# Linear attention with a gate, LoRA experts and Strassen products in one program: when masks, weights, decays and gates are loaded or computed, the order of the inner products, and which rows of out_w are loaded ahead

## The chip, the cores and the metric

The kernel runs on one core of one Trainium2 chip. The metric is the time of one execution on the device, in microseconds (us), lower is better. Times are medians of several runs; next to them stands one execution that the hardware profiler recorded, with a span and a time of its own. All data is float32.

## The reference, cut to what matters

x is 2 x 512 tokens of 512 features. After a layer norm, two branches are computed and added to x: a linear attention with decay (32 heads of 128, gated), and a dense layer with 8 LoRA experts of rank 16, of which the router takes 2 for each token. Cut down:

```python
qkv = silu(xn @ qkv_w.T)                       # 1024 tokens x 12288: q, k, v of 32 heads
def step(kv, blk):                             # over blocks of 32 tokens
    scores = einsum('bhnd,bhmd->bhnm', cq, ck) * diag_decay
    intra = einsum('bhnm,bhmd->bhnd', scores, cv)
    inter = einsum('bhnd,bhde->bhne', cq * q_decay, kv)
    kv_next = kv * block_decay + einsum('bhnd,bhne->bhde', ck * k_decay, cv)
    return kv_next, intra + inter
xf = attn * rsqrt(mean(attn * attn) + EPS)     # over all 4096 features of a token
gate = sigmoid(xn @ gate_w.T)                  # 1024 x 4096
attention = gate * (norm_w * xf) @ out_w.T     # 1024 x 4096 times 4096 x 512
out = x + attention + base(xn) + experts(xn)
```

Nearly all the arithmetic lies in five products: q, k, v and gate (each 1024 x 512 times 512 x 4096), and the last one with out_w (1024 x 4096 times 4096 x 512).

## The kernel before, in words

**Two-level fast products.** The four projections are computed by a scheme of seven products in place of eight, on two levels. The output features are cut into 16 sets n: eight for v and gate in turn (n < 8, kind 0 and 1) and eight for q and k (kind 2; one set holds four heads). A set has seven outer rounds q (1 to 7), each a combination of a set's weight blocks with a combination of xn; a round has seven inner products i (1 to 7), each four 128x256 matmuls on TensorE (`inner_product`, L292, matmuls L300 and L303). That makes 112 rounds.

- The *weights*: `load_block` (L132) loads a block of 512 KB as two DMAs of 256 KB, into a ring of five buffers `raw`. `encode` (L151) is a generator on POOL: the outer combinations L156 (128x1024) into `s`, and four inner ones (L175 to L181) into `e`. It runs two rounds ahead of its products, one step per slot.
- The *evictions*: `after(r, i)` (L336) combines a product's result out of PSUM. Products 1 and 2 accumulate into one bank `pa`, 5 and 3 into `pc`, 6 into `pb`, 7 and 4 into `pd`. After product 1, ACT copies `pa` to `pb` (L375) before product 2 adds to `pa` and product 6 to `pb`; after product 6, ACT copies `pb` to `pd` (L386) before 7 and 4 add to `pd`. Other results are added to partial sums of earlier rounds in `outer_sums`, on DVE: `put` (L354), `taken` (L369), and the one after product 7 that makes `w2` (L395). In round q = 7 the `w2` is then added twice by `put`, into the partial sum u3 and into the finished quarter (1, 1).
- A finished quarter goes through `result` (L322): Silu (L328) or Tanh (L326) on ACT. v and gate are then written to DRAM (`v_kept`, `gate_kept`). q and k stay in `qk`, a ring of five buffers; when both halves of a head and batch are there, `complete` (L474) makes an *item* of it, 64 in all.

**Attention.** `attend` (L482) is a generator for one item. Its first four steps are DMAs and one DVE operation: load the head's decays as `mask` (L488, L489: two tiles of 64 KB each, ring of four), transpose k in 32x32 blocks on DVE (L494), write them to DRAM as `k_kept` (L497), load them back as `kt` (L502, four DMAs) and load v (L504). `complete` puts these steps 1, 2, 3 and 6 slots after the item is done (L479). Then come four stages:

- A: four score matmuls (L509, bank `sc`), times the mask on DVE (`scores`, L511), the decayed q on POOL (`qd`, L514), the load of the gate (L517);
- B: the decayed k on ACT (`kd`, L521), scaled by a column of the mask;
- C: three matmuls kd by v (L527, bank `sc`), their running sums on DVE (`state`, L529 and L531);
- D: seven matmuls into bank `at` (`pa`, L537 and L539); ACT squares them into `sq` (L545), POOL adds that to `ssq` (L546), DVE multiplies with the gate (`gT`, L548). Two slots later gT is written to DRAM as `g_kept` (L550).

`stages` (L556) interleaves the items: A of item i is followed by B and C of item i - 1 and D of item i - 2, where A and B share one step of the order, and C and D have one each.

**The order.** The main loop (L667 to L721) writes the order by hand. Slot k belongs to round r0 = k // 7 and place m = k % 7; `SLOTS` (L664) names for each place how many rounds back and which inner product. A slot first issues the weight loads (at m = 0 of a set's rounds q = 5, 7 and 3 the next set's blocks are loaded, two or four DMAs in one go), then the steps that are `later`, then the inner product with its evictions, then one step of `encode`, and last a stage of attention whenever a credit that grows by 24/49 a slot has reached 1. From the first q/k round on ((VG, 1), about 406 us into the span) up to the end of the early output products (L752) this written order is each engine's order (`manual_schedule`); before and after it, a scheduler orders the instructions. Each engine works its own queue in order. All DMAs go out from SP's queue in that order too, so a DMA that waits holds the DMAs behind it.

**Output projection.** It uses seven products on one level, over 16 pairs of heads p, for two halves f of the tokens. Per pair: out_w is loaded (512 KB, L586) and scaled by norm_w on ACT (L593), the attention result is loaded (`gated`, L598), and four sums each are formed of both (`gsum` on DVE, L609; `wsum` on POOL, L610); each product is two matmuls of 128x256 (L627). Four pairs (`EARLY`) begin while attention still ends: `ENDS` (L635) has their loads by slots, L736 to L746 runs the last stages of attention with pair 3's out_w scaled at the second (`left == 1`), and the sums of pairs 1 to 3. After the written order ends, the buffers of attention are given up and a pool `gated_pool` opens, into which pairs 4 and on are loaded (L764 to L766), then the products 2, 3 and 4 of pairs 0 to 3 run. x_back (2 MB, x plus the expert branch) is loaded into a pool that opens where the buffers of the projections were (L775 to L778), at pair 8 of the first half (L816), for the last additions (L787).

Of the kernel before, what the change touches and what calls it, by code (L numbers as in the profile page):

```python
# [60 lines left out]
def attn_moe_kernel(ctx: ExitStack, tc: tile.TileContext, x, qk_w, v_w, gate_w, out_w, norm_w,  # L61
# [70 lines left out]
    def load_block(n, fo, ko):  # L132


        t = blocks[n, fo, ko] = aw.tile([P, 2, 2, 256], F32, tag="raw", name="raw", bufs=5)
        ks = slice(2 * ko, 2 * ko + 2)
        for i in range(2):
            if kind(n) == 0:
                nc.sync.dma_start(t[:, i], v_w[n - n % 2 + i][:, ks, fo * 256 : (fo + 1) * 256])
            elif kind(n) == 1:  # L140
                h = 4 * (n - n % 2) + 4 * i + 2 * fo
                nc.sync.dma_start(t[:, i], gate_w[h : h + 2, :, ks, :].rearrange("f p k d -> p f (k d)"))
            else:
                nc.sync.dma_start(t[:, :, i, :],
                                  qk_w[4 * (n - VG) + 2 * fo + i][:, :, ks, :].rearrange("p u k d -> p u (k d)"))

# [51 lines left out]
    with tc.tile_pool(name="setup", bufs=1, side="right") as sp:  # L198
# [9 lines left out]
        load_block(0, 0, 0)  # L208
        nc.sync.dma_start(wbase, base_w)
        for fo, ko in ((1, 0), (1, 1), (0, 1)):  # L210
            load_block(0, fo, ko)
        load_block(1, 0, 0)
# [97 lines left out]
    qk = {}  # L310

    def place(n, fo, to, ij):

        fi, ti = divmod(ij, 2)
        if kind(n) < 2:
            return ring("v")
        item = 4 * (n - VG) + 2 * fo + fi, to
        if item not in qk:
            qk[item] = ring("qk", [P, 2, S])
        return qk[item][:, :, ti * HB : (ti + 1) * HB]  # L320
# [15 lines left out]
    def after(r, i):  # L336
# [5 lines left out]
        def put(ij, v, more):  # L342

            for (_, to), t in zip(adds, more):
                new = isinstance(to, str)
                o = outer_sums[n, to][ij] if new else place(n, *to, ij)

                def halves(t):
                    return t.rearrange("p (u y) -> p u y", u=2) if len(o.shape) == 3 else t

                if t is None:
                    nc.scalar.copy(o, v)
                else:
                    nc.vector.tensor_tensor(o, halves(v), halves(t), ALU.add)  # L354
                if not new:
                    result(n, *to, ij, o)
# [27 lines left out]
        elif i == 6:  # L384
            st["pd"] = seeded[1 + r % 2]
            nc.scalar.copy(st["pd"], st["pb"])  # L386
            st["w"] = taken("w", st["pb"], 1)
        elif i == 3:
            put(1, st["pc"], st["w"])
        elif i == 7:  # L390
            if len(adds) == 1:
                put(3, st["pd"], st["y"])
            else:
                c = temp("w2")
                nc.vector.tensor_tensor(c, st["pd"], st["y"], ALU.add)  # L395
                put(3, c, addends(3))
        elif i == 4:
            put(2, st["pd"], addends(2))
# [83 lines left out]
    def attend(head, b):  # L482
# [3 lines left out]
        mask = work.tile([P, 2, P], F32, tag="mask", name="mask", bufs=4)  # L486

        nc.sync.dma_start(mask[:, 0, :], decay[head][:, :P])  # L488
        nc.sync.dma_start(mask[:, 1, :], decay[head][P - 1, P : 2 * P].partition_broadcast(P))  # L489
# [13 lines left out]
        v = ring("v")  # L503
        nc.sync.dma_start(v, v_kept[s_][:, u, f, b, :])  # L504
# [30 lines left out]
        for j in range(TB):  # L535
            o = pa[:, j * P : (j + 1) * P]
            mm(o, v[:, j * P : (j + 1) * P], sc[:, j, :], True, j == 0)  # L537
            if j:
                mm(o, state[:, j - 1, :], qd[:, j - 1, :], False, True)  # L539
        if b not in seen:  # L540
# [6 lines left out]
        gT = ring("gT")  # L547
        nc.vector.scalar_tensor_tensor(gT, gate, 1.0, pa, ALU.add, ALU.mult)  # L548
# [7 lines left out]
    def stages():  # L556


        for i in range(ITEMS + 2):
            if i < ITEMS:  # L560
                while i not in ready or ready[i] > now[0]:
                    yield None
                next(running[i])
            if 1 <= i <= ITEMS:
                next(running[i - 1])
            if i < ITEMS:
                yield True
            if 1 <= i <= ITEMS:
                next(running[i - 1])
                yield True  # L570
            if i >= 2:
                next(running[i - 2])
# [91 lines left out]
    SLOTS = ((0, 1), (0, 5), (0, 2), (1, 7), (0, 6), (0, 3), (1, 4))  # L664
    credit = 0.0
    in_order = ctx.enter_context(ExitStack())
    for k in range(7 * len(rounds) + 7):  # L667
        now[0] = k
        r0, m = divmod(k, 7)
        if m == 0:  # L670
# [12 lines left out]
            if r0 < len(rounds):  # L683
# [13 lines left out]
                if n + 1 < NSET:  # L697
                    for fo, ko in {5: ((0, 0),), 7: ((1, 0), (1, 1)), 3: ((0, 1),)}.get(q, ()):
                        if (n + 1, fo, ko) not in blocks:
                            load_block(n + 1, fo, ko)  # L700
# [3 lines left out]
        if r0 == len(rounds) and SLOTS[m][0] == 0:  # L704
            if m == 0:
                sums[0].update({1: bank("fr"), 6: bank("fr"), 5: seeded[0], 7: seeded[1]})
            early_product()
        back, i = SLOTS[m]
# [9 lines left out]
        if items:  # L718
            credit = min(credit + 24 / 49, 1.5)
            if credit >= 1 and next(stage):  # L720
                credit -= 1  # L721
# [14 lines left out]
    for left, _ in enumerate(stage):  # L736
# [3 lines left out]
        if left == 1:  # L740
            scale_out_w(3)
        for _ in range(2 if left == 0 else 1):
# [21 lines left out]
    load_gated(0, EARLY)  # L764
    for p in range(EARLY, EARLY + 2):
        next_out_w(p, gated_pool)  # L766
# [8 lines left out]
    last_products.close()  # L775
    projections.close()
    late = right("late")
    x_back = late.tile([P, NT, HID], F32, tag="x_back", name="x_back")  # L778
# [30 lines left out]
    for i, (f, p) in enumerate(todo):  # L809
        if i + 1 < len(todo):  # L810
# [5 lines left out]
        if (f, p) == (0, NP // 2):  # L816
            nc.sync.dma_start(x_back, x_kept)
# [71 lines left out]
```

## Time and profile before

| what | value |
|---|---|
| runs | 1183.01, 1188.82 and 1192.49 us; median 1188.82 us |
| profiled execution | 1193.15 us, span 1191.4 us |
| mean granted clock of TensorE | 0.995 |
| ACT: Silu of q and k, L328 | 128 times, 630 ns each |
| ACT: copy `pa` to `pb`, L375 | 112 times, 575 ns each |
| ACT: copy `pb` to `pd`, L386 | 112 times, 575 ns each |
| DVE: gT, L548 | 64 times, 684 ns each |
| DVE: `w`, L369 | 110 times, 688 ns each |
| POOL: ssq, L546 | 62 times, 1272 ns each |
| POOL: qd, L514 | 64 times, 1017 ns each |
| POOL: outer combinations, L156 | 32 times, 2366 ns each |
| POOL: idle before qd, ended by the mask's DMA | 45.4 us in all |
| DVE: idle before gT, ended by ACT's square | 81.6 us in all |
| DMA: moved by all queues | 197.15 MB, mean 165 GB/s |
| DMA: weights of q and k, 64 issues of 256 KB | 4.9 us median from issue to landing |

The durations are means of one instruction in the profiled execution. "Idle before" is time in which the engine stood, put down to what ended the wait; it costs time only where TensorE then has to wait too. Queue time of an engine or of its instruction sequencer is written with a q or the ending ld: SPq is the queue from which DMAs are issued, PEld is the loading of matmul weights, which runs beside the matmuls. `ps_fr`, `ps_sc`, `ps_at` and `sd` are PSUM banks: two, two, one and three of them.

### The profile page before, as it was taken

To read this page: it belongs to the slowest core of one execution; us is meant where nothing else is said; L and a number is where in the kernel's file an instruction comes from. 1 tells how busy PE (TensorE), PEld (TensorE's weight loads), DVE (VectorE), ACT (ScalarE), POOL (GpSimd) and SP (SyncE) were. 2 spreads that over 40 slices of the span, in tenths; PEclk is the share of its full clock that TensorE was granted. 3 is DMA by queue.
4 is the path that set the end of the run, shared out by engine and by line. 5 is a ranking of instruction groups with operands and counts; after the bars stand their busy time and mean duration, and the time that the engine had idled before them with its cause. 6 is when DMAs were issued, how large, how long until landed. Compare 5 with 4: busy or idle time off the path is not lost.

```text
span 1191.4 us, 18113 instructions
## 1 busy us (share of the span) xinstructions
PE 1144.7 (96%) x6024; PEld 994.0 (83%) x6024; DVE 759.9 (64%) x1350; ACT 435.1 (37%) x772; POOL 737.7 (62%) x798
## 2 busy tenths in 40 slices
PE   6999999999999999999999998999989989899998
PEld 5578888888888878989989897988979878788887
DVE  7477766666675666667767766676666753636333
ACT  3244444434534434344343433434333431330000
POOL 5266977757767656657576765757766544655452
PEclk9999999999999999999999999999999999999999
DMA  7335465344444345555656656565566672864221
GB/s 242 114 107 183 153 212 194 127 157 161 142 140 151 124 145 172 167 177 173 193 178 188 180 156 207 158 194 164 168 199 168 214 226 91 328 212 125 89 89 53
DMA packets 188717, 197.15 MB, mean 165 GB/s; under 512 B 50128, under 2 KB 159696, under 8 KB 188368
## 3 DMA queue, kind: packets, MB, share of 16 engines
q1 hardware_dynamic: 188624, 195.98, 52.5%
q8 instruction: 49, 0.80, 0.3%
q14 instruction: 44, 0.36, 0.1%
HBM read 126.16 MB, written 69.76 MB: 164 GB/s over the span
## 4 chain that ended last, share of the span: by engine, by line
PE 67%; DVE 8%; DMA 6%; issue 3%; ACT 3%; SPq 2%; POOL 2%; DVEq 0%; ACTq 0%; POOLq 0%
PE ps_fr L303 14%; PE sd L303 13%; PE sd L627 5%; PE ps_at L89 5%; PE ps_sc L89 5%; PE sd L300 5%; PE ps_fr L627 4%; PE ps_sc L627 4%; PE ps_sc L303 4%; PE ps_fr L300 3%; DMA mask<-in_decay 3%; PE ps_sc L300 3%; DVE qk L354 2%; DVE sum L354 2%; PE ps_at L627 1%
## 5 line engine op out<-in xcount | busy, mean ns | idle before, releaser
L328 ACT ACTIVATE qk<-qk 128x512 f32<-128x512 f32 x128 | 80.6, 630 | 252.6 <-DVE qk L354 252.5
L303 PE MATMUL sd<-xt,e 128*128 128x256 f32 x672 | 166.8, 381 | 0.0
L546 POOL TENSOR_TENSOR ssq<-ssq,sq 128x512 f32<-128x512 f32 x62 | 78.9, 1272 | 126.4 <-ACT sq L545 116.9
L303 PEld LDWEIGHTS sd<-xt,e 128*128 128x128 f32 x672 | 125.1, 192 | 15.0
L369 DVE TENSOR_TENSOR w<-sd,sum 128x512 f32<-128x512 f32 x110 | 74.4, 688 | 72.0 <-ACT sd L386 71.0
L548 DVE SCALAR_TENSOR_TENSOR gT<-gate,ps_at 128x512 f32<-128x512 f32 x64 | 43.8, 684 | 89.4 <-ACT sq L545 81.6
L514 POOL TENSOR_TENSOR qd<-qk,mask 128x384 f32<-128x384 f32 x64 | 65.1, 1017 | 47.8 <-DMA mask<-in_decay 45.4
L610 POOL TENSOR_TENSOR wsum<-wo 128x256 f32<-128x256 f32 x56 | 46.2, 841 | 74.6 <-PE sd L627 34.6
L175 POOL TENSOR_TENSOR e<-s 128x256 f32<-128x256 f32 x64 | 46.8, 730 | 70.4 <-PE sd L303 49.9
L89 PE MATMUL ps_at<-scores,v 128*128 128x128 f32 x512 | 89.2, 277 | 0.0
L375 ACT COPY sd<-ps_fr 128x512 f32<-128x512 f32 x112 | 64.4, 575 | 48.2 <-PE ps_fr L300 23.4
L609 DVE TENSOR_TENSOR gsum<-gated 128x256 f32<-128x256 f32 x56 | 26.9, 521 | 85.0 <-PE ps_sc L627 71.1
L89 PEld LDWEIGHTS ps_at<-scores,v 128*128 128x128 f32 x512 | 78.2, 193 | 3.4
L156 POOL TENSOR_TENSOR s<-raw 128x1024 f32<-128x1024 f32 x32 | 75.7, 2366 | 2.7 <-DMA raw<-in_v_w 2.7
L303 PE MATMUL ps_fr<-xsum,s 128*128 128x256 f32 x288 | 75.4, 385 | 1.0 <-ACT sd L375 0.9
L89 PE MATMUL ps_at<-qd,state 128*128 128x128 f32 x384 | 74.6, 276 | 0.0
L386 ACT COPY sd<-sd 128x512 f32<-128x512 f32 x112 | 64.4, 575 | 23.0 <-PE sd L303 17.2
L175 POOL TENSOR_TENSOR e<-raw 128x256 f32<-128x256 f32 x48 | 35.6, 741 | 59.5 <-PE sd L303 32.6
L89 PEld LDWEIGHTS ps_sc<-qk 128*128 128x128 f32 x512 | 67.8, 193 | 3.4
L89 PE MATMUL ps_sc<-qk 128*128 128x128 f32 x512 | 68.0, 276 | 0.0
L303 PE MATMUL ps_fr<-xt,e 128*128 128x256 f32 x224 | 58.2, 382 | 9.8 <-DVE qk L354 9.8
L326 ACT ACTIVATE v<-v 128x512 f32<-128x512 f32 x64 | 40.4, 631 | 73.7 <-DVE v L354 69.1
(299 smaller groups left out, 2888.3 us busy)
## 6 DMA issues: line engine op xcount, KB each, us to landing
v_kept<-v SPq DMA_DIRECT2D x64, 256.0 KB, 2.5
gate_kept<-v SPq DMA_DIRECT2D x64, 256.0 KB, 2.5
raw<-in_qk_w SPq DMA_DIRECT2D x64, 256.0 KB, 4.9
v<-v_kept SPq DMA_DIRECT2D x64, 256.0 KB, 2.9
gate<-gate_kept SPq DMA_DIRECT2D x64, 256.0 KB, 3.9
g_kept<-gT SPq DMA_DIRECT2D x64, 256.0 KB, 3.5
gated<-g_kept SPq DMA_DIRECT2D x28, 512.0 KB, 3.7
k_kept<-squares SPq DMA_DIRECT2D x64, 192.0 KB, 4.1
```

What stands on the lines that cost most here:

```text
L89: nc.tensor.matmul(o, lhsT, rhs, start=start, stop=stop)
L156: nc.gpsimd.tensor_tensor(t, a, b, op)
L175: nc.gpsimd.tensor_tensor(e[:, 0], a21, a22, ALU.add)
L300: nc.tensor.matmul(o.rearrange("p (g j d) -> p j g d", g=2, j=2)[:, u], x_[:, u * P : (u + 1) * P], a, start=first and u == 0, stop=True, ...
L303: nc.tensor.matmul(o[:, u * HB : (u + 1) * HB], a[:, u], x_, start=first and u == 0, stop=True, skip_group_check=True)
L328: nc.scalar.activation(v, v, AF.Silu)
L369: nc.vector.tensor_tensor(o, v, t, ALU.add)
L375: nc.scalar.copy(st["pb"], st["pa"])
L386: nc.scalar.copy(st["pd"], st["pb"])
L514: nc.gpsimd.tensor_tensor(qd, q[:, P:].rearrange("p (j n) -> p j n", j=TB - 1), mask[:, 1, :].unsqueeze(1).to_broadcast([P, TB - 1, P]), A ...
L546: nc.gpsimd.tensor_tensor(ssq[b], ssq[b], sq, ALU.add)
L627: nc.tensor.matmul(sums[n][:, i * HO : (i + 1) * HO], l[:, i * P : (i + 1) * P], r, start=p == 0 and i == 0, stop=p == NP - 1, skip_group_ ...
```

## The change

It has eight parts. In the diff, the first `yield` stands in the loop over a block's two DMAs.

1. *Weights by halves.* `load_block` becomes a generator that yields after each DMA of 256 KB; the main loop takes one at each even place m, in place of up to four at m = 0.
2. *Masks.* An item's mask is loaded in `place`, when its first result gets its buffer, and no longer by `attend`'s first step after both results are there.
3. *v.* v is loaded in `attend`'s first step, where the mask was, and no longer after kt.
4. *SLOTS.* Product 7 of the round before moves one place ahead of product 2: 1, 5, 7, 2, 6, 3, 4 in place of 1, 5, 2, 7, 6, 3, 4.
5. *Decays ahead of products.* A slot that will run stage B (kd on ACT) issues it ahead of its inner product and evictions; A, C and D stay behind them. In `stages`, B is now taken on the first `next`, the rest on the second, told apart by `yield False`.
6. *Gates ahead of squares.* In stage D, gT on DVE is issued before ACT's square. Both read the bank `at`.
7. *One addition on POOL.* In round q = 7, the addition of `w2` to u3 runs on POOL; both of its inputs are in SBUF. It runs 16 times.
8. *Six pairs preloaded.* In the last stages, pair 3's out_w is scaled at `left == 5` in place of `left == 1`; there out_w of pairs 4 and 5 is loaded, into a pool that exists already, and pair 4's `gated` into a `raw` buffer. The pools of the projections are closed at pair 6 in place of ahead of the loop, and x_back is loaded there in place of at pair 8; its memory is then that of buffers which pair 4's products and sums still use.

```diff
 def load_block(n, fo, ko):
...
+            yield
+    def load_blocks(n, *of):
+        for fo, ko in of:
+            if (n, fo, ko) not in blocks:
+                yield from load_block(n, fo, ko)
...
+    def load_mask(head):
+        mask = work.tile([P, 2, P], F32, tag="mask", name="mask", bufs=4)
+        nc.sync.dma_start(mask[:, 0, :], decay[head][:, :P])
+        nc.sync.dma_start(mask[:, 1, :], decay[head][P - 1, P : 2 * P].partition_broadcast(P))
+        return mask
...
         if item not in qk:
             qk[item] = ring("qk", [P, 2, S])
+            masks[item] = load_mask(item[0])
...
-        def put(ij, v, more):
+        def put(ij, v, more, in_sbuf=False):
...
-                    nc.vector.tensor_tensor(o, halves(v), halves(t), ALU.add)
+                    engine = nc.gpsimd if new and in_sbuf else nc.vector
+                    engine.tensor_tensor(o, halves(v), halves(t), ALU.add)
...
-                put(3, c, addends(3))
+                put(3, c, addends(3), in_sbuf=True)
...
-        mask = work.tile([P, 2, P], F32, tag="mask", name="mask", bufs=4)
-        nc.sync.dma_start(mask[:, 0, :], decay[head][:, :P])
-        nc.sync.dma_start(mask[:, 1, :], decay[head][P - 1, P : 2 * P].partition_broadcast(P))
+        mask = masks.pop((head, b))
+        v = ring("v")
+        nc.sync.dma_start(v, v_kept[s_][:, u, f, b, :])
         yield
...
-        v = ring("v")
-        nc.sync.dma_start(v, v_kept[s_][:, u, f, b, :])
...
+        gT = ring("gT")
+        nc.vector.scalar_tensor_tensor(gT, gate, 1.0, pa, ALU.add, ALU.mult)
         if b not in seen:
...
-        gT = ring("gT")
-        nc.vector.scalar_tensor_tensor(gT, gate, 1.0, pa, ALU.add, ALU.mult)
...
         for i in range(ITEMS + 2):
             if i < ITEMS:
                 while i not in ready or ready[i] > now[0]:
                     yield None
-                next(running[i])
             if 1 <= i <= ITEMS:
                 next(running[i - 1])
             if i < ITEMS:
+                yield False
+                next(running[i])
                 yield True
             if 1 <= i <= ITEMS:
+                yield False
                 next(running[i - 1])
                 yield True
             if i >= 2:
+                yield False
                 next(running[i - 2])
...
-    SLOTS = ((0, 1), (0, 5), (0, 2), (1, 7), (0, 6), (0, 3), (1, 4))
+    SLOTS = ((0, 1), (0, 5), (1, 7), (0, 2), (0, 6), (0, 3), (1, 4))
...
-                if n + 1 < NSET:
-                    for fo, ko in {5: ((0, 0),), 7: ((1, 0), (1, 1)), 3: ((0, 1),)}.get(q, ()):
-                        if (n + 1, fo, ko) not in blocks:
-                            load_block(n + 1, fo, ko)
+                weights = load_blocks(n + 1, *{5: ((0, 0),), 7: ((1, 0), (1, 1)), 3: ((0, 1),)}.get(q, ())
+                                      if n + 1 < NSET else ())
+        if m % 2 == 0:
+            next(weights, None)
...
+        begun = None
+        if items:
+            credit = min(credit + 24 / 49, 1.5)
+            if credit >= 1:
+                begun = next(stage)
         back, i = SLOTS[m]
...
-        if items:
-            credit = min(credit + 24 / 49, 1.5)
-            if credit >= 1 and next(stage):
-                credit -= 1
+        if begun is False:
+            next(stage)
+            credit -= 1
...
-    for left, _ in enumerate(stage):
+    for left, _ in enumerate(begun for begun in stage if begun):
...
-        if left == 1:
+        if left == 5:
             scale_out_w(3)
+            for p in (4, 5):
+                load_out_w(p, early_pool.tile([P, 2, HID], F32, tag=f"wo{p}", name="wo"))
+            load_gated(0, 4, end_buffer("raw", [2, B, HT]))
...
-    load_gated(0, EARLY)
-    for p in range(EARLY, EARLY + 2):
-        next_out_w(p, gated_pool)
+    for p in (4, 5):
+        scale_out_w(p)
...
-    last_products.close()
-    projections.close()
-    late = right("late")
-    x_back = late.tile([P, NT, HID], F32, tag="x_back", name="x_back")
...
     for i, (f, p) in enumerate(todo):
+        if (f, p) == (0, 6):
+            last_products.close()
+            projections.close()
+            late = right("late")
+            x_back = late.tile([P, NT, HID], F32, tag="x_back", name="x_back")
+            nc.sync.dma_start(x_back, x_kept)
...
-        if (f, p) == (0, NP // 2):
-            nc.sync.dma_start(x_back, x_kept)
```

More of the change, by code (lines that the diff above doesn't have):

```diff
@@ L207, in attn_moe_kernel @@
                 nc.sync.dma_start(wra, router_a_w)
-        load_block(0, 0, 0)
+        for _ in load_block(0, 0, 0):
+            pass
         nc.sync.dma_start(wbase, base_w)
-        for fo, ko in ((1, 0), (1, 1), (0, 1)):
-            load_block(0, fo, ko)
-        load_block(1, 0, 0)
+        for _ in load_blocks(0, (1, 0), (1, 1), (0, 1)):
+            pass
+        for _ in load_block(1, 0, 0):
+            pass
         nc.sync.dma_start(nw, norm_w)
@@ L309, in attn_moe_kernel @@
              2: [("x1", (0, 0))], 3: [("u4", (0, 1))], 4: [("u3", (1, 0))]}
-    qk = {}
+    qk, masks = {}, {}
+    def load_mask(head):
[3 more added lines that the diff above has]
+        return mask
     def place(n, fo, to, ij):
```

## The prediction

> **What bounds the kernel now.** First the page, part 1: TensorE is the full engine, the others have room.
>
> ```profile
> PE 1144.7 (96%) x6024; PEld 994.0 (83%) x6024; DVE 759.9 (64%) x1350; ACT 435.1 (37%) x772; POOL 737.7 (62%) x798
> ```
>
> Busy time hides short stalls, so I read matmul starts in the timeline. Back to back, a 128x256 matmul starts 0.216 us after the last (a product has four: 0.86 us), a 128x128 one 0.112, a 128x512 one 0.429, a 128x136 one 0.116. At that pace 4032, 1832 (with the 16 of one column), 80 and 64 of them need 1119.6 us. Added up over the trace, start to start, 56.9 us go beyond that pace: 3.1 before 56 us (setup), 9.2 up to 406 us (v and gate sets), 31.7 up to 960 us (q/k sets with attention), 12.8 up to 1020 us (passage to the output projection), none afterwards. No edit can win more than this. By what ended them: ACT's copy L375 21.4 (8.1 in the v/gate part, 13.1 in the q/k part, 0.2 in setup), DVE's additions L354 11.8, ACT's kd L521 5.2, POOL's wsum 3.3, the scaled out_w (L593) 3.3, other DVE work 2.3, a v load 0.8, no semaphore 8.8 (part of it half clock). The waits of TensorE name the same ones (total, times, longest):
>
> ```profile
> PE ps_fr L303 <- ACT sd L375: 9.9, 12, 2.0
> PE ps_fr L303 <- DVE qk L354: 9.8, 6, 3.3
> PE ps_fr L627 <- ACT wo L593: 3.0, 1, 3.0
> PE ps_sc L89 <- ACT kd L521: 2.5, 2, 2.1
> ```
>
> Why is DVE late? The chain of waits at 503 to 515 us (start, length, what):
>
> ```profile
> 503.24 0.55 SPq L144
> 503.78 0.04 issue
> 503.83 0.61 SPq L144
> ...
> 505.79 7.15 DMA mask<-in_decay
> ...
> 513.03 0.06 DVE scores L511
> 513.10 0.55 issue
> 513.64 0.68 DVE sum L354
> 514.32 0.61 DVE qk L354
> 514.93 0.14 issue
> 515.07 2.60 PE ps_fr L303 x8
> ```
>
> Four weight loads of 256 KB go out in one burst, the mask queues behind them and lands 7.15 us after issue, L511 holds DVE, DVE's additions come late, and TensorE waits for their bank. The timeline of the passage shows the other kind:
>
> ```profile
> 977.79 1.33 ACT L593 ACTIVATE e<-e,nw 128x512 f32<-128x512 f32 x2 [6.13 <-DMA e<-in_out_w]
> 980.15 0.74 PEld L89 LDWEIGHTS ps_sc<-v,kd 128*128 128x128 f32 x6 [2.46 <-ACT kd L521]
> ```
>
> ACT stands 6.13 us before the scaling of pair 3's out_w, and square and kd behind it in its queue hold TensorE.
>
> **The change part by part.** The sum starts from the profiled execution: 1193.15 us (span 1191.4 and 1.75 around it), 4.3 above the median of the runs shown, 1188.82.
>
> *Product 7 moved (SLOTS).* Product 2 accumulates into the bank that L375 copies (575 ns); between products 1 and 2 lay product 5 alone, 0.86 us; now 7 too, 1.73 us. Cutting each stall by 0.86 leaves 2.8 of the 21.4. I take 17 off, 1.6 less than that, for the ACT delay below; bounds 0 (the copy is late anyhow) and 21.4. Product 2's result, its DVE addition (0.69) and Silu (0.63) come a slot later; its bank is wanted again three products (2.6 us) on: nothing. POOL waits for product 7 before it refills an operand buffer (L175 <- L303 and L300, 117 us in all); that ends a slot sooner, off the path: nothing.
>
> *Masks.* Same 128 DMAs of 64 KB, issued with the first result instead of a slot after the second: 3 slots earlier for one head of a pair, 5 for the other. A slot of the q/k part is 554 us / 392 = 1.41 us, so 4.2 and 7.1 us earlier, against longest waits of 6.2 (POOL) and 4.0 (DVE). The four buffers are held longer: the load now comes at least 6 slots (8.5 us) behind the kd of the item four back, for the last two items 1 and 0, where SP, and the k_kept, kt and weight loads behind it, may stand up to 1.4 us. Of the 10.7 us that DVE's additions cost in the q/k part I take 9.5; bounds 0 and 10.7.
>
> *Weights by halves.* The four 256 KB issues (2.5 us of SP at once) go to slots 0, 2, 4, 6: this helps the masks. The last half leaves 8.5 us later; its first use is 8 slots (11 us) after that, its landing 4.9. Only set 1 of the first two uses it in the next round; POOL stood idle 3.5 and 4.0 us there. Nothing; bounds 0 and 4.9.
>
> *v loads* move on SP from behind kt to before k_kept; their buffer was freed at least 7 slots before. The one stall on v goes: 0.8; bounds 0.8 gained and, by one 0.43 us issue ahead of 64 kt groups if all show, 28 lost. I take the gain: kt waits for k_kept's landing anyway (177 us of SP).
>
> *kd ahead of the product's evictions.* In the q/k part kd costs TensorE 2.9; I take 2.4. From kt's landing to kd's start the trace has 1.0 us at the lowest quartile and 2.3 in the middle; moved up by one or two evictions of 0.6, some 16 of 64 kd would hold ACT up to 1.0 us, with the L375 and L386 copies behind, which now have 1.73 us. Bounds 2.9 gained, 16 lost.
>
> *Gate ahead of square.* Both read one PSUM bank and the program orders them. DVE no longer waits for ACT (81.6 us, 51 times); ACT waits for DVE. By the trace the square starts 0.1 us (median) after the last matmul of its bank; then it needs DVE's 0.69 first: 0.7 later, 1.2 with the 0.47 that DVE is busy on average. Behind it on ACT stand the next copies, on POOL ssq (1.27) and the operands. Only where this stage falls right before an L375, about 9 of 64, does it reach product 2: the 1.6 above. Bounds 0 and 64 x 0.73 = 47 lost.
>
> *One addition to POOL*, 16 times: 16 x 1.27 (the ssq row) = 20 us more on POOL, which idles 450, and 12.8 less on DVE. POOL then waits for DVE's w2, with operands for two rounds later behind it: a round of slack (10 us). Nothing, bounds 17 gained (DVE) and 20 lost. The row speaks against this one: additions with both inputs in SBUF are longer than those with one in PSUM,
>
> ```profile
> L354 DVE TENSOR_TENSOR sum<-w,sum 128x512 f32<-128x512 f32 x16 | 12.8, 802 | 0.5
> L354 DVE TENSOR_TENSOR v<-w,sum 128x512 f32<-128x512 f32 x8 | 9.2, 1147 | 0.0
> L354 DVE TENSOR_TENSOR v<-ps_sc,w 128x512 f32<-128x512 f32 x32 | 21.9, 685 | 1.5
> ```
>
> and now POOL's addition and DVE's remaining one are released by the same w2. If DVE stands for POOL's whole 1.27, the pair takes 1.27 + 0.69 = 1.96 instead of 0.80 + 0.75 or 1.15: 8 x 0.41 + 8 x 0.01 = 3.4 us lost. The Trainium skill ("SBUF — State Buffer", Who interferes with whom) says just this: a VectorE instruction with two SBUF inputs and a GpSimd one that reads SBUF exclude each other for the whole instruction. By that rule the sum is 1160, without it 1156; the long 1147 row agrees with it.
>
> *Passage.* Pair 3 is scaled at the sixth stage, after its load has landed: of the 7.9 us lost from 977 to 992 (half of it at half clock) I take 5, since POOL's ssq and wsum remain. The loads of pairs 4 and 5 go out some 17 us sooner; of the 3.7 lost at 1016 to 1018 I take 3.4. Against it, ssq starts 0.7 later before wsum, four times at most: 1 lost. The saved memory ties x_back to the end of pair 4's products, with pair 8's out_w behind it on SP: 18 us until pair 8, against 9.1 and at most 11.1 for landing, 0.7 for scaling and 1.6 for wsum: hidden by some 4 us; bounds 0 and 7 (2 MB moved first).
>
> *Half clock.* It was granted for 3.4 us after the stall at 513 us: 1.7 gained without that stall (the other drop is in the 7.9).
>
> Sum: 17 + 9.5 + 0.8 + 2.4 + 5 + 3.4 - 1 + 1.7 = 38.8; 2 off for new small waits: 36.8. 1193.15 - 36.8 = **1156**; own range 1148 to 1163.
>
> **Rivals.**
> 1. *The copies stay late.* At 596 us two Silus and a square stood before L375; DVE sets their pace. Then masks, v and passage alone pay, 9.5 + 0.8 + 7.4 = 17.7: **1175** (1167 to 1183). For: ACT waits 252 us for L354. Against: the v/gate stalls average 0.17 us, far under 0.86. 0.20.
> 2. *SP falls behind*: masks and v before kt delay each by up to 1.3 us (three issues of 0.43), over the slack of a quarter of kd: 16 x 1.3 = 21: **1177**. Against: the same issues leave later places. 0.10.
> 3. *Slower: ACT waits for DVE at every square* and TensorE for ACT behind it: 1156 + 47 = **1203**. It decides from 37 / 0.73 = 50 of 64 items. For: ACT is one queue. Against: ACT idles 63%, and two products cover. 0.07.
> 4. *Nearly all stalls go*: 1193.15 - 56.9 + 3.1 + 3 = **1142**. 0.06.
> 5. *Lock between POOL and DVE*, 3.4 lost: **1160**, 0.10, within the forecast's range.
>
> **How the numbers follow.** Forecast 0.57 (the lock's 0.10 within), rivals 0.20, 0.10, 0.07, 0.06. About 1% (1177 to 1201) is what a measurement can tell from no change. Faster: 0.57 + 0.06 + 0.12 of rival 1 + 0.03 of rival 2 = 0.78; same 0.08 + 0.07 = 0.15; slower 0.07. The range 1145 to 1179 leaves out most of rival 4, rival 3, and the upper ends of 1 and 2, about 0.19.
>
> **What would show it.** Right: no mask wait on POOL or DVE above 1 us; TensorE's waits for the copy below 5 us; none for out_w; ACT's square waiting for gT some 50 times and DVE's gT for PE; PEclk never below 9. Wrong: new TensorE waits for L375's or L386's copies with a square before them, kd waiting for kt more than ten times, SP standing before a mask load, a gap at pair 8, or DVE's remaining two-input addition near 1.9 us with TensorE idle behind it.

## The result and the profile after

The changed kernel takes 1155.97 us, median of 5 runs (1151.59 to 1156.68), against 1188.82 before (5 runs, 1183.01 to 1196.04): the ratio is 0.971, 95% interval 0.968 to 0.974. The forecast was 1156. The profiled execution went from 1193.15 to 1156.46 us, its span from 1191.4 to 1154.7.

Part 1 of the page after, the line of the engines, shows TensorE fuller, DVE a little relieved and POOL a little busier:

```profile
PE 1130.3 (98%) x6024; PEld 997.9 (86%) x6024; DVE 753.9 (65%) x1334; ACT 434.1 (38%) x772; POOL 755.7 (65%) x814
```

The waits of TensorE after, past the setup (total, times, longest); L392 is the old L375, L371 the old L354, L535 kd, L628 wsum, L645 the output products:

```profile
PE sd L645 <- POOL wsum L628: 3.4, 3, 1.9
PE ps_fr L311 <- ACT sd L392: 2.5, 8, 1.0
PE ps_fr L311 <- DVE qk L371: 0.9, 2, 0.8
PE ps_at L89 <- POOL ssq L562: 0.7, 1, 0.7
PE ps_fr L645 <- POOL wsum L628: 0.6, 1, 0.6
```

The copy went from 9.9 in this view to 2.5, DVE's addition from 9.8 to 0.9, the scaled out_w (3.0) is gone. What is left at the top is wsum, in the passage to the output projection.

The waits of SP show a thing that I had not looked for. L502 before and L518 after are kt's loads, L513 after is the writing of k_kept:

```profile
SPq L502 <- DMA k_kept<-squares: 176.8, 55, 5.5
```

```profile
SPq L518 <- DMA k_kept<-squares: 53.9, 34, 3.0
SPq L513 <- DVE squares L510: 50.6, 31, 3.6
```

Before, SP mostly stood for k_kept to land; now it is early, and stands for DVE's transpose too. From the end of the transpose to the issue of k_kept it took 2.09 us before (median of 64) and takes 0.03 now; from the end of the transpose to kt's landing it took 10.15 us and takes 8.04.

I use one measure for all runs: matmul starts beyond the back-to-back pace (1118 us in every kernel; the prediction has 1119.6, but its own figures for each shape add up to 1118, and no other number of it rests on that sum), in the profiled execution, put down to what ended them. "Copy" is L375, "additions" are all waits for DVE, "passage" is what comes after the last inner product; all in us. The times are medians, and a profiled execution can lie some us off its median: that of the kernel before took 1193.15 us, that of masks early alone 1191.34. Each later group of runs had the kernel before beside it again, at 1193.26, 1192.77 and 1192.44 us; the ratios go by these. The changed kernel was timed in the first group alone, so a difference of less than about 5 us to its 1155.97 rests on the stalls more than on the times.

| kernel | time | stalls | copy | kd | additions | rest | passage | setup |
|---|---|---|---|---|---|---|---|---|
| before | 1188.82 | 56.9 | 21.3 | 2.9 | 11.8 | 4.9 | 12.8 | 3.1 |
| changed | 1155.97 | 20.4 | 5.5 | 0 | 1.3 | 0.3 | 9.9 | 3.4 |
| changed, old SLOTS | 1176.34 | 40.6 | 25.7 | 0 | 1.6 | 1.6 | 8.3 | 3.4 |
| changed, masks late | 1182.32 | 45.2 | 9.2 | 7.4 | 6.3 | 7.3 | 12.0 | 2.9 |
| changed, weights in bursts | 1155.58 | 19.3 | 6.0 | 0.7 | 1.3 | 0.2 | 8.3 | 2.9 |
| changed, square first | 1160.80 | 25.9 | 9.1 | 0 | 1.3 | 1.0 | 11.6 | 3.0 |
| changed, kd behind | 1170.53 | 34.4 | 2.4 | 18.6 | 1.5 | 0.1 | 8.3 | 3.4 |
| changed, masks late and kd behind | 1185.38 | 46.1 | 4.0 | 23.5 | 2.2 | 1.5 | 11.8 | 3.2 |
| changed, addition on DVE | 1166.02 | 29.5 | 13.2 | 0 | 4.0 | 1.0 | 8.3 | 3.1 |
| before, new SLOTS alone | 1185.52 | 50.6 | 2.5 | 16.9 | 10.4 | 2.5 | 15.2 | 3.1 |
| before, masks early alone | 1182.83 | 55.8 | 26.1 | 1.3 | 4.6 | 13.6 | 7.4 | 2.9 |
| before, kd ahead alone | 1191.31 | 57.5 | 23.3 | 0 | 10.5 | 7.6 | 12.3 | 3.8 |
| changed, ssq late in the passage | 1152.75 | 17.2 | 6.2 | 0 | 1.3 | 0.3 | 6.4 | 3.1 |
| the same, qd and square late too | 1149.03 | 13.0 | 5.6 | 0 | 1.3 | 0.2 | 2.8 | 3.1 |

### The profile page after: what moved, and what is told of

Same layout as the page of the kernel before. It is cut to its first block, busy times and chain, and to the rows that moved or that the text cites. A ratio compares the mean times of both kernels' runs of the same rounds, so it can differ in the third digit from the quotient of the medians.

```text
span 1154.7 us, 18210 instructions
## 1 busy us (share of the span) xinstructions
PE 1130.3 (98%) x6024; PEld 997.9 (86%) x6024; DVE 753.9 (65%) x1334; ACT 434.1 (38%) x772; POOL 755.7 (65%) x814
## 4 chain that ended last, share of the span: by engine, by line
PE 81%; DVE 7%; issue 4%; DMA 3%; POOL 2%; ACT 2%; SPq 1%; DVEq 0%; ACTq 0%; POOLq 0%
PE ps_fr L311 17%; PE sd L311 15%; PE ps_at L89 7%; PE ps_sc L89 7%; PE sd L308 6%; PE sd L645 5%; PE ps_sc L645 5%; PE ps_fr L645 4%; PE ps_fr L308 4%; PE ps_sc L308 4%; PE ps_sc L311 4%; PE sd L89 2%; DVE qk L371 2%; DVE sum L371 1%; PE ps_at L645 1%
## 5 line engine op out<-in xcount | busy, mean ns | idle before, releaser
L311 PE MATMUL sd<-xt,e 128*128 128x256 f32 x672 | 172.6, 379 | 0.0
L344 ACT ACTIVATE qk<-qk 128x512 f32<-128x512 f32 x128 | 80.4, 630 | 215.1 <-DVE qk L371 212.2
L311 PEld LDWEIGHTS sd<-xt,e 128*128 128x128 f32 x672 | 123.6, 190 | 14.6
L628 POOL TENSOR_TENSOR wsum<-wo 128x256 f32<-128x256 f32 x56 | 45.5, 829 | 72.8 <-PE sd L645 34.7
L392 ACT COPY sd<-ps_fr 128x512 f32<-128x512 f32 x112 | 64.8, 578 | 42.3 <-PE ps_fr L311 22.5
L627 DVE TENSOR_TENSOR gsum<-gated 128x256 f32<-128x256 f32 x54 | 24.2, 489 | 83.7 <-PE ps_sc L645 67.1
L555 DVE SCALAR_TENSOR_TENSOR gT<-gate,ps_at 128x512 f32<-128x512 f32 x64 | 43.6, 681 | 45.4 <-PE ps_at L89 37.7
L561 ACT ACTIVATE sq<-ps_at 128x512 f32<-128x512 f32 x62 | 37.0, 597 | 86.7 <-DVE gT L555 86.5
L528 POOL TENSOR_TENSOR qd<-qk,mask 128x384 f32<-128x384 f32 x64 | 64.3, 1004 | 1.9 <-PE ps_at L89 1.9
L342 ACT ACTIVATE v<-v 128x512 f32<-128x512 f32 x64 | 40.4, 631 | 65.9 <-DVE v L371 64.8
L344 ACT ACTIVATE v<-v 128x512 f32<-128x512 f32 x64 | 40.3, 631 | 56.7 <-DVE v L371 53.6
```

The source lines that it names most:

```text
L311: nc.tensor.matmul(o[:, u * HB : (u + 1) * HB], a[:, u], x_, start=first and u == 0, stop=True, skip_group_check=True)
L344: nc.scalar.activation(v, v, AF.Silu)
L392: nc.scalar.copy(st["pb"], st["pa"])
L528: nc.gpsimd.tensor_tensor(qd, q[:, P:].rearrange("p (j n) -> p j n", j=TB - 1), mask[:, 1, :].unsqueeze(1).to_broadcast([P, TB - 1, P]), A ...
```

## The experiments

### Parts undone one at a time

**Old SLOTS.**

```diff
-    SLOTS = ((0, 1), (0, 5), (1, 7), (0, 2), (0, 6), (0, 3), (1, 4))
+    SLOTS = ((0, 1), (0, 5), (0, 2), (1, 7), (0, 6), (0, 3), (1, 4))
```

> The changed kernel with the old SLOTS (product 7 behind product 2 again). Theory A (the terms are separate, each cures stalls of its own): the copy after product 1 again has one product of cover, 0.86 us, and TensorE loses about the 21 us to it that it lost before, in place of 5.7: 1156 + 15 = 1171 us, the stalls put down to the copy between 18 and 24 us, those for DVE's additions below 3. Theory B (one cause: late masks and bursts made ACT and DVE late, and with them the copy): the copy's stalls come back by less than 6 us, 1156 to 1162.

Measured: 1176.34 us, ratio 0.984 (0.978 to 0.990). The copy's stalls are 25.7, a little over theory A's 24, and the time is 5 us over its 1171; the additions stay at 1.6. Theory A holds: one more product of cover is what cured the copy.

**Masks late, weights in halves.**

```diff
-            masks[item] = load_mask(item[0])
...
-        mask = masks.pop((head, b))
+        mask = load_mask(head)
```

> The changed kernel with each mask loaded in attention's first step again, ahead of v; the weights stay in halves. Theory A: the early load is what took the mask's wait from DVE; the mask lands late in some heads again, and DVE's additions hold TensorE some 10 us: 1166 us. Theory B: the burst of four weight loads was what made the mask late, and the halves alone cure it: no wait for a mask over 1.5 us on DVE or POOL beside the last items, 1155 to 1158.

Measured: 1182.32 us, ratio 0.989 (0.985 to 0.994): 26 us lost, where A said 10 and B nothing. B falls. A has the direction, but the mask's own wait on DVE is not the whole. ACT's and POOL's waits in this run:

```profile
ACT kd L534 <- DMA kt<-k_kept: 25.5, 15, 3.8
```

```profile
POOL qd L527 <- DMA mask<-in_decay: 23.1, 12, 3.5
```

The second line is the late mask. The first has grown (it was 3.0 before the change, and the changed kernel has no such line): kt is late. On SP the two mask loads and v now stand ahead of k_kept; it is issued 4.57 us after the transpose (median, 2.09 before), and kt lands 12.80 us after the transpose.

**Weights in bursts.**

```diff
-        if m % 2 == 0:
-            next(weights, None)
+        if m == 0:
+            for _ in weights:
+                pass
```

> The changed kernel with the weights loaded in bursts of up to four at place 0 again, masks early. Theory A (the early load is enough: 4 to 7 us earlier against waits up to 6.2): at most one or two us of stalls more, 1155 to 1159. Theory B (the burst is the cause, and now the v load ahead of k_kept stands behind it too): kt and with it kd come late, 1162 to 1168.

Measured: 1155.58 us, ratio 0.967 (0.963 to 0.972), kt 8.24 us after the transpose. The bursts cost nothing once the masks are early: A.

**Square ahead of the gate.**

```diff
-        gT = ring("gT")
-        nc.vector.scalar_tensor_tensor(gT, gate, 1.0, pa, ALU.add, ALU.mult)
         if b not in seen:
...
             nc.gpsimd.tensor_tensor(ssq[b], ssq[b], sq, ALU.add)
+        gT = ring("gT")
+        nc.vector.scalar_tensor_tensor(gT, gate, 1.0, pa, ALU.add, ALU.mult)
         yield
```

> The changed kernel with the square ahead of the gate again. Theory A (the changed trace: in the passage POOL's ssq, and behind it wsum, waits for a square that itself waits 0.8 us for the gate): the gate's place costs there about 0.7 us at each of four waits and half a clock gate, and 1 to 2 us in the main part; without it 1150 to 1153 us, passage stalls of 6 to 8 us in place of 9.9. Theory B (the gate's place is what brought DVE on time: DVE idled 82 us behind the square before): DVE's additions come late again and TensorE loses 5 to 10 us to them: 1161 to 1166.

Measured: 1160.80 us (1157.98 to 1161.37), ratio 0.971 (0.966 to 0.976). The median is 4.8 over the changed kernel's, while the two ratios are alike; the stalls decide. A falls: the passage got no cheaper (11.6). There the first two waits, 0.6 and 1.2 us for wsum, did shrink to 0.3 (for gsum) and 0.5, but the scheduler had moved an output product (number 4 of pair 2, which lies behind the end of the written order) ahead, and TensorE waited 3.1 us for that product's wsum; so this run does not price the gate's place in the passage. B has the direction, but not the place: the additions stay at 1.3, it is the copy that grows, from 5.5 to 9.1 (in the three other kernels that differ from the changed one only in the weights or in the passage it is 5.6 to 6.2). The waits of DVE, ACT and TensorE in this run:

```profile
DVE gT L562 <- ACT sq L559: 76.2, 48, 2.6
```

```profile
ACT qk L344 <- DVE qk L371: 252.7, 119, 3.5
```

```profile
PE ps_fr L311 <- ACT sd L392: 5.0, 7, 1.0
```

DVE stands for the square again (81.6 us before the change), its additions come later, the Silus wait 252.7 us for them (252.5 before, 212.2 in the changed kernel), and the copy stands behind those: once in each set, 0.82 us against 0.37.

**kd behind the product and its evictions**, in the order A then B of before.

```diff
-            if 1 <= i <= ITEMS:
-                next(running[i - 1])
             if i < ITEMS:
                 yield False
                 next(running[i])
+            if 1 <= i <= ITEMS:
+                next(running[i - 1])
+            if i < ITEMS:
                 yield True
```

> The changed kernel with kd behind its slot's product and evictions again (the order of before, A then B in one step). Theory A: kd holds TensorE for 2.4 to 3 us in the q/k part again, nothing else moves: 1158 to 1160 us. Theory B (kd's early place pays through the stalls of others, since kd then stood behind copies and Silus): 1162 or more.

Measured: 1170.53 us, ratio 0.983 (0.979 to 0.988): 14.6 lost, so A falls and B holds. The timeline of this run, first, and of the changed kernel at the same place:

```profile
576.83 1.29 DVE L371 TENSOR_TENSOR qk<-w,sum 128x512 f32<-128x512 f32 x1
578.15 0.63 ACT L344 ACTIVATE qk<-qk 128x512 f32<-128x512 f32 x1 [1.93 <-DVE qk L371]
578.68 0.60 ACT L535 ACTIVATE kd<-kt,mask 128x384 f32<-128x384 f32 x1
579.34 0.94 PE L89 MATMUL ps_sc<-v,kd 128*128 128x128 f32 x6 [1.28 <-ACT kd L535]
```

```profile
571.09 0.61 ACT L535 ACTIVATE kd<-kt,mask 128x384 f32<-128x384 f32 x1
571.81 1.28 DVE L371 TENSOR_TENSOR qk<-w,sum 128x512 f32<-128x512 f32 x1
573.11 0.83 PE L89 MATMUL ps_sc<-v,kd 128*128 128x128 f32 x6
573.12 1.23 ACT L344 ACTIVATE qk<-qk 128x512 f32<-128x512 f32 x2 [1.43 <-DVE qk L371]
```

ACT has nothing to do for 1.93 us, but kd stands behind a Silu that waits for DVE's addition. Issued ahead, kd is done 1.4 us before its matmuls. kt is never what kd waits for: the least time from kt's landing to kd is 0.99 us in the changed kernel (lowest quartile 3.2).

**The addition to u3 on DVE again.**

```diff
-                put(3, c, addends(3), in_sbuf=True)
+                put(3, c, addends(3))
```

> The changed kernel with the addition to u3 on DVE again. Theory A (hidden on both engines, the lock between POOL and DVE costs DVE's own addition 0.6 us in the seven rounds where both run, which nothing waits for): 1155 to 1158, same as the changed kernel. Theory B (the lock costs TensorE): faster by 3, 1153. Theory C (the 13 us that DVE is relieved of are needed): slower, 1160 or more, with more stalls for DVE's additions or the copies after Silus.

Measured: 1166.02 us, ratio 0.979 (0.976 to 0.983), 10 lost: C. The timeline of this run, and of the changed kernel, at the two additions that read w2:

```profile
507.21 1.27 POOL L562 TENSOR_TENSOR ssq<-ssq,sq 128x512 f32<-128x512 f32 x1 [4.06 <-ACT sq L561]
507.68 1.36 DVE L371 TENSOR_TENSOR sum<-w,sum 128x512 f32<-128x512 f32 x1
508.45 1.18 POOL L181 TENSOR_TENSOR e<-raw 128x256 f32<-128x256 f32 x1
508.96 1.21 DVE L371 TENSOR_TENSOR qk<-w,sum 128x512 f32<-128x512 f32 x1
```

```profile
503.48 1.28 POOL L562 TENSOR_TENSOR ssq<-ssq,sq 128x512 f32<-128x512 f32 x1 [4.05 <-ACT sq L561]
504.02 1.29 DVE L371 TENSOR_TENSOR qk<-w,sum 128x512 f32<-128x512 f32 x1
504.71 1.73 POOL L371 TENSOR_TENSOR sum<-w,sum 128x512 f32<-128x512 f32 x1
```

An addition of DVE with both inputs in SBUF that starts while POOL is in an instruction takes some 0.55 us longer than what is left of that instruction, in place of 0.68 in all: 1.29 with 0.74 left, 1.36 with 0.81, and 2.45 with 1.91 left (174.44 us, changed kernel). The one that starts first keeps its time and POOL's grows: at 436.57 us the changed kernel's took 0.69 on DVE, and the one on POOL, 0.04 later, 1.79 in place of 1.27. With both on DVE each one meets POOL, 2.57 us together; before the change, in seven of the eight q/k sets, POOL had at most 0.05 us left or began after them, and they took 0.69 and 0.68. What I priced at nothing takes 1.3 us a set from the chain that TensorE waits for: the stall at the copy is 1.07 us a set in this run, and 0.37 with the addition on POOL.

**Two at once: masks late and kd behind**, by the two diffs above.

> The changed kernel with late masks (as in the run with late masks alone, 1182 us, where the sum of my terms gave 1166) and with kd behind the evictions again. Theory A (the two moves depend on each other: an early kd stands at the head of ACT's queue, waits there for kt, which the late masks delayed through DVE, and holds copies and Silus behind it): taking kd back makes it faster than 1182, about 1156 + 10 + 3 = 1169 us, with ACT's waits of kd for kt under 8 us in place of 25.5. Theory B (late masks alone cost 26 us, by way of DVE and SP, whatever kd does): 1180 to 1185.

Measured: 1185.38 us, ratio 0.993 (0.990 to 0.996). B: with late masks, kd's place is worth about 3 us (the runs spread from 1175.85 to 1188.02), while it is worth 14.6 with early ones. ACT waits less for kt, though not under 8 us as A had it, and TensorE waits 23.5 us for kd:

```profile
ACT kd L534 <- DMA kt<-k_kept: 14.6, 9, 2.9
```

The prices don't add up: alone 26.4 and 14.6, together 29.4.

v's place (part 3) and the pairs preloaded (part 8) were not undone by themselves; that TensorE no longer waits for out_w is read from the trace of the changed kernel alone.

### Parts done alone, on the kernel before

**New SLOTS alone** (the diff above turned round).

> The kernel before with the new SLOTS alone. Theory A (each edit has a price of its own, that of undoing it): 20 us faster, ratio 0.983, the copy's stalls from 21 down to 5. Theory B (the edits share their slack; a stall that goes uncovers what was late behind it): the copy's stalls go as in A, but those for kd and DVE's additions, 2.9 and 11.8 us before, grow, and the gain is 8 to 14 us, ratio 0.988 to 0.993.

Measured: 1185.52 us, ratio 0.9925 (0.989 to 0.996), a gain of 7 us by the medians and 9 by the ratio. B. The copy's stalls fall to 2.5, and others take their place:

```profile
PE ps_sc L89 <- ACT kd L521: 13.9, 10, 3.2
PE ps_fr L303 <- DVE qk L354: 9.1, 7, 2.4
```

**Masks early alone.** `load_mask` is called in `place`, as in the change; nothing else.

> The kernel before with the masks loaded early alone (weights in bursts, v and all else as before). Theory A: 26 us faster, ratio 0.978. Theory B: 9 us or less, ratio 0.992 to 1.0, DVE's additions below 3 us of stalls.

Measured: 1182.83 us, ratio 0.992 (0.988 to 0.996); the profiled execution is one of the longer ones (1191.34). The additions fall from 11.8 to 4.6, not below 3, and the gain is at B's upper edge. Now the copy holds TensorE 1.80 us in every set:

```profile
PE ps_fr L303 <- ACT sd L383: 15.7, 13, 1.9
PE ps_fr L303 <- DVE qk L362: 2.4, 7, 0.4
```

**kd ahead alone.**

```diff
+        begun = None
+        if items:
+            credit = min(credit + 24 / 49, 1.5)
+            if credit >= 1:
+                begun = next(stage)
         back, i = SLOTS[m]
...
-            if credit >= 1 and next(stage):
-                credit -= 1
+        if begun is False:
+            next(stage)
+            credit -= 1
```

> The kernel before with kd ahead of the slot's product alone. Theory A: 14 us faster, ratio 0.988. Theory B: kd's 2.9 us at best, and with late masks and kt a loss is as likely: ratio 0.997 to 1.005, ACT waiting for kt 10 times or more.

Measured: 1191.31 us, ratio 0.998 (0.995 to 1.001): B, no change that this measurement can tell. kd's stalls go, the copy's grow by 2.0 and those without a semaphore, half clock among them, by more. ACT now waits for kt 10 times, 6.4 us in all (3 times and 3.0 before), as B had it; with kt early, in the changed kernel, it never does.

### A faster version

**ssq behind wsum in the passage.** In the last stages, POOL's addition to ssq is put off until that step's part of wsum is issued, and the written order ends behind the products 2, 3 and 4 of pairs 0 to 3.

```diff
-            nc.gpsimd.tensor_tensor(ssq[b], ssq[b], sq, ALU.add)
+            def add_square():
+                nc.gpsimd.tensor_tensor(ssq[b], ssq[b], sq, ALU.add)
+            if tail:
+                put_off.append(add_square)
+            else:
+                add_square()
...
             next(more, None)
+        while put_off:
+            put_off.pop()()
         early_product()
...
-    in_order.close()
     attention.close()
...
             rms = inv_sqrt(gated_pool, pr[:, : B * TB], B * TB, "rms", 1.0 / (H * D))
+    in_order.close()
```

> The changed kernel with two edits in the passage alone: POOL adds each late square to ssq behind that slot's part of wsum, no longer ahead of it, and the written order goes on up to the products 2, 3 and 4 of the first four pairs, so that the scheduler can't move these. Theory A (in the passage POOL's ssq stands ahead of wsum and TensorE waits for that): the waits for wsum, 5.2 us, fall under 1.5 and a drop of the clock (1.7) may go: 1150 to 1152 us. Theory B (POOL has too much work there: qd or ssq is late in place of wsum): passage stalls of 8 or more, 1154 to 1158.

Measured: 1152.75 us, ratio 0.968 (0.965 to 0.972); passage 6.4. A's direction, half its size by the stalls; the times alone (1151.78 to 1153.97) don't tell it from the changed kernel. wsum keeps 2.8, because the decayed q stands before it on POOL in its turn, and kd's wait grew to 2.7.

**And the decayed q and the late square.** POOL's L528 is put off in the same way, and ACT's square of an item (but the last two) is issued behind the next step's kd.

```diff
+            def square():
...
+            squares_left.append(square) if tail and (head, b) in items[:-2] else square()
...
+        put_off.append(decayed_q) if tail else decayed_q()
...
     for left, _ in enumerate(begun for begun in stage if begun):
+        for f in old_squares:
+            f()
+        old_squares[:] = squares_left
+        squares_left.clear()
...
+        while put_off:
+            put_off.pop(0)()
```

> The faster version of the passage (1152.75 us: wsum ahead of ssq, written order kept on) with two further edits there: the decayed q on POOL goes behind wsum too, and each late square on ACT goes behind the next item's kd. Theory A: the 2.8 us for wsum and 2.7 for kd that were left in the passage fall to about 1.5 in all, 1148 to 1150 us. Theory B (ACT's square and POOL's decayed q are needed soon: the bank of the attention result and its last matmuls wait for them): nothing gained, 1152 to 1155.

Measured: 1149.03 us, ratio 0.960 (0.956 to 0.965): A. The waits of TensorE past the setup:

```profile
PE ps_fr L311 <- ACT sd L392: 2.3, 7, 1.1
PE ps_fr L311 <- DVE qk L371: 1.0, 2, 0.8
PE sd L652 <- DVE gsum L634: 0.9, 2, 0.7
PE ps_at L89 <- ACT sq L564: 0.6, 1, 0.6
PE ps_fr L308 <- ACT sd L392: 0.5, 1, 0.5
PE ps_sc L89 <- ACT kd L537: 0.2, 1, 0.2
```

It beats the changed kernel: the two ratio intervals lie apart (0.956 to 0.965, and 0.968 to 0.974). Against this, the two were not timed side by side; their runs, 1147.82 to 1149.57 and 1151.59 to 1156.68 us, do not overlap.

## Why the prediction was right, and where its terms were not

The sum was right because it was a count of TensorE's stalls, and most of them went: 36.5 us by the table, 36.8 forecast. Outside the passage 10.5 of 44.1 us are left, 3.4 of them in the setup. Term by term, forecast and difference of the two traces:

| term | forecast | traces |
|---|---|---|
| product 7 (copy) | 17 | 15.8 |
| masks (additions) | 9.5 | 10.5 |
| v | 0.8 | 0.8 |
| kd | 2.4 | 2.9 |
| passage | 5 + 3.4 - 1 | 2.9 |
| half clock and the rest outside it | 1.7 | 3.8 |
| new small waits (in the traces: setup) | -2 | -0.3 |

That the median came out at the forecast to a tenth of a us is luck: 4.5 us too many for the passage and 1.2 for the copy stand against 5.3 too few in other rows, and the prediction started from the profiled execution of before, 4.3 us above that median. And the right terms do not make the parts right that were to earn them, as follows.

*Passage: mis-sized.* The 3.4 for the loads of pairs 4 and 5 came; out_w is waited for no more. The 5 for pair 3 did not: the waits for wsum grew from 3.3 to 5.2, and the half clock there stayed, 6.83 us of it in one drop before and in two of 3.41 after. My cost for the gate there, ssq 0.7 later and "1 lost", counted the delay and not the queue. The timeline of the changed kernel:

```profile
950.35 0.69 DVE L555 SCALAR_TENSOR_TENSOR gT<-gate,ps_at 128x512 f32<-128x512 f32 x1 [1.26 <-PE ps_at L89]
951.13 0.60 ACT L561 ACTIVATE sq<-ps_at 128x512 f32<-128x512 f32 x1 [6.91 <-DVE gT L555]
951.80 1.27 POOL L562 TENSOR_TENSOR ssq<-ssq,sq 128x512 f32<-128x512 f32 x1 [3.43 <-ACT sq L561]
953.03 0.91 POOL L628 TENSOR_TENSOR wsum<-s 128x256 f32<-128x256 f32 x1
953.99 1.13 PE L645 MATMUL sd<-wsum,gsum 128*128 128x256 f32 x4 [1.92 <-POOL wsum L628]
```

POOL was idle 3.43 us, waited for a square that waited for the gate, and only then took up wsum, which needed neither. The two faster versions, which put such work behind wsum, show it: 9.9 to 2.8.

*Gate ahead of square: wrong sign.* I priced only ACT's new wait (1.6 within the 17). DVE's wait for ACT, 81.6 us, I named as removed and gave no value; undone, it costs 3.6 us of stalls at the copy (4.8 us by the medians). DVE was the later of the two, as ACT's waits for its additions show (252.7 us undone, 212.2 with the gate ahead).

*One addition to POOL: "nothing" was wrong.* The rows of before showed pairs that in the q/k part mostly met no POOL work, and held for their place in time only; the lock that I feared for the pair of DVE and POOL acts on two additions of DVE too. The move was worth 10 us in the end. The Trainium skill ("SBUF — State Buffer", Who interferes with whom) says that a VectorE instruction with two SBUF inputs and a GpSimd one that reads SBUF exclude each other; the doubled 1.29 and 1.36 agree. My use of the page against this change was the wrong way round: the addition that stays on DVE would have met POOL anyway.

*Masks: right for a reason and a half.* They land in time (DVE's 15.6 us of mask waits at L511 are gone, and POOL's 45.4 at qd), but they also took two issues out of the way of k_kept and kt, which I had passed over with "kt waits for k_kept's landing anyway". This delay of kt, beside the mask's own wait, is what the trace shows behind the 26 us that late masks cost in the changed kernel. v, which in that run is loaded ahead of k_kept too, has a share in it: with late masks kt lands 12.80 us after the transpose with v ahead, and 10.15 with v behind kt (the kernel before, which differs in other parts too); with early masks it is 8.04 and 7.56 (masks early alone). What that share is worth in time stays open.

*kd: the margin was misread.* Paired for all 64 items, kt lands 2.3 us (lowest quartile) and 5.0 us (median) before kd starts in the trace of before, not 1.0 and 2.3; seven of the 64 lie below 1.0. So the bound of 16 lost was too wide. The 2.4 fits kd's own stalls of before (2.9), but not what kd's place is worth beside the other parts: undone from the changed kernel, TensorE waits 18.6 us for kd, much as with SLOTS alone (16.9).

*The terms are not prices of the edits.* Alone, the three largest gain 0.75%, 0.8% and 0.2% by the ratios, some 9, 9 and 2 us; undone from the changed kernel they cost 20, 26 and 15. Once in each set, DVE's additions after product 7, the Silus after those and the copy or kd behind them form one chain, and TensorE waits for whichever end of it is worst. Where one end is cured the other shows (kd, 2.9 to 16.9, after SLOTS alone). My rival 1, "the copies stay late" (1175), is near to what the traces show with another part missing: the copy's stalls are 13.2 us with the addition on DVE (1166) and 9.2 with late masks (1182). I gave it 0.20 without seeing that parts which I had put at nothing decide it.

Of the signs named in advance: TensorE's waits for the copy are 3.0 us in the view of its waits, for out_w none, ACT's square waits for gT 54 times, no gap at pair 8. The view still puts three waits of POOL before ssq, 1.6 us each, down to a mask's load; ssq reads no mask, and each of them ends 0.1 us or less after the square that it adds. The clock sign failed: two drops of 3.41 us each, both in the passage behind the waits for wsum and ssq.

## What to carry to other kernels

A stall in a trace has a price in that schedule only: where several engines feed one chain, list what would be late next behind each cured stall, and expect that edits pay little alone and much together. When you cost a wait that is added to an in-order queue, count all that stands behind it and does not need it, as wsum behind ssq. Count what a move takes away from an engine as carefully as what it adds, and ask which of the two engines was the later one.

## What the runs showed of the hardware

In the run with masks early alone, TensorE stalls 1.80 us once in each set of 71.7 us, and in the profiled execution the granted clock falls to 0.5 for 3.41 us after seven of the eight such stalls, at 526.61, 598.29, 669.97 us and so on, 71.68 apart (the first, at 456.20, was not followed). That is 23.9 us at half speed, so some 12 us lost; the trace has 11.9 us of stalls without a semaphore. Ten executions of this kernel fall into two groups, 1181.4 to 1183.2 us with a mean clock of 0.997 to 0.999, and 1189.1 to 1193.5 with 0.989 to 0.992. In the run with SLOTS alone, four stalls of 1.68 us in the same part were followed by no drop. The Trainium skill ("TensorE: Matmul & The Clock Gate", Part 1) says that the clock falls after at least one idle window of about 3.4 us, and that the window runs freely; the traces agree with the 3.41 us, 71.68 is 21 of them, but here a stall of half a window was enough. That the two groups come from where the window stands at the start is argued, not shown.
